# Message passing on one core: row limits compared on VectorE straight from PSUM, two transposes moved from TensorE to DMA, and a new instruction order

## The chip, the cores and the metric

The kernel runs on one core of a Trainium2 chip. The metric is the device time of one launch in microseconds, given as the median of several runs. One further execution was recorded by the hardware profiler. All durations of single instructions below come from that execution.

The core has five instruction streams. TensorE (PE in the profile; its weight loads are listed apart, as PEld) multiplies matrices and writes to PSUM. VectorE (DVE) and ScalarE (ACT) work elementwise and can read PSUM. GpSimd (POOL) works elementwise on SBUF. SyncE (SP) only issues DMAs here. Each stream executes its own instructions strictly in the order in which the program emits them, and waits on semaphores where it needs another stream's result.

## What is computed

There are 128 graphs of 128 nodes with 64 features. The reference, cut to what matters:

```python
# layer 0, per graph
mask = adj > 0
h  = relu((x @ W1a)[:, None, :] + (x[:, None, :] - x[None, :, :]) @ W1b + b1)   # node pair (j, k), 192 wide
hm = sum over k of h[j, k] * mask[j, k]
x  = layernorm(x + hm @ W2 + deg[:, None] * b2)          # deg = row sums of mask
# layer 1, per graph
m   = relu(relu(x @ V1 + c1) @ V2 + c2)
msg = relu(adj @ m)
x   = layernorm(x + GRU(msg, x))                          # three gates, 64 wide each
```

The mask is sparse: a row's neighbours are picked one by one, and only the picked pairs are computed.

## The kernel before

**Groups.** The 128 graphs are worked off in 32 groups of four (`G = 4`). For a group, `masks`, `ranks`, `degrees` and `counts` make the 0/1 mask, a running count of neighbours along each row (`rankT`), the row sums and, for each row, how many extra segments it needs (`nseg`). `values0` and `pieces` project `x` (the second one into three bf16 pieces `b0`, `b1`, `b2`).

**Picking neighbours.** Each row has a fixed number of first slots (`W0 = 8`, in two halves) and, where it has more neighbours, extra segments of `W1 = 4` slots. `pick0` builds 0/1 selection matrices on VectorE by comparing `rankT` with slot numbers. `gather0` multiplies these with the pieces on TensorE: 12 small matmuls a step and 16 steps a group. Each result lies in a PSUM tile `pv` that ScalarE has filled beforehand with the row's own part (`seed0`). `keep0` on ScalarE and `reduce` on VectorE (line 666, `acc`) apply the relu and add the results up. `pick1`, `gather1`, `seed1`, `keep1` and `reduce1` do the same for the extra segments. There are three `pv` buffers.

**Offsets, owners and places.** The extra segments of all rows are packed one after the other. `offsets` multiplies `nseg` by triangular matrices, which gives in PSUM (`po`) each row's first and last position. ScalarE copies the last position to `off` (line 458) and scales the first into `woff` (line 460). GpSimd then compares a ramp `iota` with `off`, once for each of the four graphs (`till`, line 466). A further matmul (`pp`) turns `till` into `own`, the 0/1 matrix that says which row owns a segment, and ScalarE copies `own` out twice (bf16 and f32).

`turned` transposes `rankT` with four TensorE transposes (`pr`, line 487) and copies the result to `rank` on ScalarE (line 490). `places` uses `rank`, `own` and `woff` (TensorE, `ps`, lines 504 to 511; ScalarE, `place`). `owners` transposes `own` in the same manner (`pq`, line 495; `ownT`, line 498), and `sums` uses `ownT` to add the segments' sums onto their rows.

**The rest.** `together` and `joined` (GpSimd) add the partial sums; `second` to `update` are layer 0's second matrix, the layernorms, layer 1 and the gates. The result of a group is stored by SP at the end of `update` (line 743).

**PSUM.** Apart from the three `pv` buffers there is a pool `ps_w` of two buffers with one tag, `w`. Every other matmul result passes through these two in turn: `pc`, `pd`, `po`, `pp`, `pr`, `pq`, `ps`, `pu`, `pz`, `ph`, `pw`, `pt`, `pm`, `pn`, `pa` and `pg`. The next matmul to use a buffer waits until the former content has been read.

**Order.** The order of the whole program is written out. Every step of every part of a group (a part is a generator, a step runs to its next `yield`) has a number in `TIMETABLE`. A step of group g has the time g times 100000 plus that number. Steps are emitted in the order of these times, and so interleave about six groups on every engine:

```python
for t in sorted(plan):
    for run in plan[t]:
        next(run, None)
```

`FIRST` and `SETUP` give other numbers for the first group and for the constants. The numbers fix an order and no durations.

Of the kernel before, what the change touches and what calls it, by code (L numbers as in the profile page):

```python
# [8 lines left out]
F32 = mybir.dt.float32  # L9
BF16 = mybir.dt.bfloat16  # L10
I32 = mybir.dt.int32
AF = mybir.ActivationFunctionType
ALU = mybir.AluOpType
AX = mybir.AxisListType

N = 128
# [3 lines left out]
G = 4  # L20
# [8 lines left out]

PER = 100000  # L30
TIMETABLE = {
    "load": (-268618,), "masks": (-266066,), "ranks": (-232900, -232900), "degrees": (-257102, -254423),
    "turned": (-224742, -220574), "counts": (-234901,), "offsets": (-217678, -211964, -197704, -192380, -189932),
    "owners": (-35894, -35894), "places": (-179586, -177714),
    "pieces": (-221915, -212465, -212465, -212025, -212025, -210034, -207896, -206287, -204509, -201502, -201502),
    "others": (-93885, -63613), "values0": (-168677, -168312, -168312), "pick0": (-187243, -177588, -157318, -147219),
    "pick1": (-101562, -99096), "over0": (-86465, -86465), "over2": (-91716, -89070), "base0": (-71690,),
    "base1": (-115079,), "base2": (-74898,), "base3": (-66289,), "together0": (-90368, -86071, -54801),
    "sums0": (-16639, -16639, -6895), "joined0": (-42043,), "joined2": (-9054,),
    "together1": (-31159, -22707, -22707), "together2": (-54332, -29252, -26680), "sums2": (-10324, -7550, -6743),  # L40
    "together3": (-14410, -11697, -11388), "second": (1322, 1729, 6614, 12070, 12714, 14947), "turn": (17589, 19125),
    "message1": (22148, 22871), "message2": (24221, 25357), "message3": (34134, 47496),
    "gates": (52002, 52335, 59212, 59212, 60471, 61641),
    "update": (63484, 134926, 134926, 146356, 147450, 212137, 231447, 236648, 276814),
    "seed0": (-137838, -111380, -107532, -90909, -89996, -88760, -70167, -48540),
    "gather0": (-132826, -123102, -109699, -102053, -101463, -95122, -90696, -82750, -82750, -77811, -77618, -69952,
        -66122, -48012, -38905, -32104), "keep0": (-129922, -97944, -81962, -65602),
    "reduce": (-116740, -102949, -100299, -89511, -89215, -81357, -75312, -71801, -69013, -44762, -33692, -24596),
    "seed1": (-80653, -43141), "gather1": (-77673, -72671, -67801, -55447, -41338, -33923, -28108, -20295),
    "keep1": (-76545, -38998), "reduce1": (-70927, -59829, -52180, -31003, -23063, -16037),  # L50
}


SETUP = (-227883, -212853, -185033, -155144, -101231, 22249)
FIRST = {
    "load": (-236749, -176840), "masks": (-192323,), "ranks": (-160512, -153527), "degrees": (-172354, -159518),
    "turned": (-108605, -102394), "counts": (-146837,), "offsets": (-115482, -109556, -106790, -103472, -99536),
    "places": (-98687, -93949),
    "pieces": (-169807, -166786, -164278, -164278, -164278, -164278, -158634, -152826, -143767, -142875, -113691),
    "values0": (-148521, -139633, -130220), "pick0": (-141784, -133982, -133982, -103074), "pick1": (-92485, -74065),  # L60
    "over0": (-88306, -87641),
}


# [1 line left out]
def adj_resnorm_kernel(  # L66
# [19 lines left out]
    nc = tc.nc  # L86
# [6 lines left out]
    ident_h = const.tile([N, N], BF16, name="ident_h")  # L93
# [13 lines left out]
    iota = const.tile([N, N], BF16, name="iota")  # L107
# [24 lines left out]
    def each(t, n):  # L132

        return t.rearrange("p (o c) -> p o c", o=1).to_broadcast([t.shape[0], n, t.shape[1]])
# [95 lines left out]
    def wide(t, n, w=F):  # L230
        return t.rearrange("p (g o) -> p g o", o=1).to_broadcast([N, n, w])
# [152 lines left out]
    with ExitStack() as fast:  # L384
        loads = fast.enter_context(tc.tile_pool(name="loads", bufs=4))
        prep = fast.enter_context(tc.tile_pool(name="prep", bufs=2))
# [3 lines left out]
        ps_w = fast.enter_context(tc.tile_pool(name="ps_w", bufs=2, space=bass.MemoryType.PSUM))  # L390
# [19 lines left out]
        def prep_parts(s):  # L410
            g = s["g"]
# [39 lines left out]
            def offsets():  # L451

                p = ps_w.tile([N, 2, G], F32, tag="w", name=f"po{g}")
                for c, m in enumerate((strict, incl)):
                    nc.tensor.matmul(p[:, c, :], m, s["nseg"], start=True, stop=True)
                yield
                off = prep.tile([N, G], F32, tag="off", name=f"off{g}")
                nc.scalar.copy(off, p[:, 1, :])  # L458
                s["woff"] = prep.tile([N, G], BF16, tag="woff", name=f"woff{g}")
                nc.scalar.mul(s["woff"], p[:, 0, :], 2.0 * W1)  # L460
                yield


                s["till"] = prep.tile([N, G, N], BF16, tag="till", name=f"till{g}")
                for i in range(G):
                    nc.gpsimd.tensor_scalar(s["till"][:, i, :], iota, off[:, i : i + 1], None, ALU.is_lt)  # L466
                yield
                p = s["po"] = ps_w.tile([N, G, N], F32, tag="w", name=f"pp{g}")
                nc.tensor.matmul(p, step, s["till"], start=True, stop=True)
                yield  # L470
                s["own"] = prep.tile([N, G, N], BF16, tag="own", name=f"own{g}")
                nc.scalar.copy(s["own"], s["po"])
                s["own32"] = prep.tile([N, G, N], F32, tag="own32", name=f"own32_{g}")
                nc.scalar.copy(s["own32"], s["po"])  # L474
# [7 lines left out]

            def turned():

                p = ps_w.tile([N, G, N], BF16, tag="w", name=f"pr{g}")
                for i in range(G):
                    nc.tensor.transpose(p[:, i, :], s["rankT"][:, i, :], ident_h)
                yield
                s["rank"] = prep.tile([N, G, N], BF16, tag="rank", name=f"rank{g}")
                nc.scalar.copy(s["rank"], p)  # L490

            def owners():
                p = ps_w.tile([N, G, N], BF16, tag="w", name=f"pq{g}")
                for i in range(G):
                    nc.tensor.transpose(p[:, i, :], s["own"][:, i, :], ident_h)
                yield
                s["ownT"] = prep.tile([N, G, N], F32, tag="ownT", name=f"ownT{g}")
                nc.scalar.copy(s["ownT"], p)

            def places():  # L500

# [62 lines left out]
            def pieces():  # L564
# [16 lines left out]

            return {
                "masks": masks, "ranks": ranks, "degrees": degrees, "counts": counts, "offsets": offsets,
                "turned": turned, "owners": owners, "places": places, "pieces": pieces, "others": others,
                "pick0": pick0, "pick1": pick1, "values0": values,
            }
# [159 lines left out]
        name, g, run = "setup", -1, setup(ps_g, ps_w)  # L746
        for t in SETUP:
            plan.setdefault(t, []).append(run)
        for g in range(ng):
            s = states[g]  # L750
# [24 lines left out]
    with ExitStack() as slow:  # L775
# [10 lines left out]
        with tc.If(flag > N):  # L786
            with tc.For_i(0, NB, 1) as b:
                bs = bass.ds(b, 1)

                s = {"name": "d", "adjT": one.tile([N, G, N], F32, name="d_adjT")}  # L790
# [23 lines left out]
                for c in range(2):  # L814
                    k = cs[c].stop
                    for what, at in ((u, c * N), (v, H + c * N)):
                        p = ps_o.tile([N, N], F32, tag="d", name="d_p")
                        nc.tensor.matmul(p[cs[c]], wall[0:F, at : at + k], dxT[:, 0, :], start=True, stop=True)
                        t = one.tile([k, N], F32, name=f"d_uv{at}")
# [5 lines left out]
                    t = one.tile([k, N], F32, name=f"d_nu{c}")  # L825
# [12 lines left out]
                for c in range(2):  # L838
                    t = one.tile([cs[c].stop, N], F32, tag=f"nd{c}", name="d_nd")
# [52 lines left out]
```

## Time and profile before

| | |
|---|---|
| median of 3 runs | 966.71 us (966.35 to 967.72) |
| profiled execution: time | 966.97 us |
| profiled execution: span, first to last instruction | 965.2 us |
| PE busy | 907.4 us, 94% of the span |
| DVE busy | 827.3 us, 86% |
| ACT busy | 841.4 us, 87% |
| POOL busy | 840.7 us, 87% |
| granted TensorE clock, mean | 0.980 of full speed |
| DMA, mean rate | 25 GB/s |

In the profile a "group" is all instructions of one line, engine and shape, with their number, busy time and mean duration in ns. An entry such as `<-PE pv L636` names what ended the idle time before an instruction. "issue" is idle time that nothing in the profile explains. SPq is SP's DMA queue.

### The profile page before, as it was taken

How to read it: one execution, taken by the hardware profiler on the slowest of the kernel's cores; microseconds unless marked ns; L12 is line 12 of the kernel's file. 1: busy time of each engine (PE TensorE's matmuls, PEld its weight loads, DVE VectorE, ACT ScalarE, POOL GpSimd, SP SyncE). 2: the span in 40 equal slices, each digit the busy share in tenths (PEclk: the TensorE clock that was granted, in tenths of full speed). 3: DMA queues.
4: the chain of work that ended last, by engine and by line, in shares of the span. 5: the costliest groups of instructions: out<-in, count | busy, mean ns of one | idle time of the engine just before them, and what ended most of it. 6: DMA issues, size and time to landing. Idle time of an engine off the chain costs nothing.

```text
span 965.2 us, 32667 instructions
## 1 busy us (share of the span) xinstructions
PE 907.4 (94%) x13333; PEld 723.1 (75%) x13335; DVE 827.3 (86%) x1586; ACT 841.4 (87%) x1762; POOL 840.7 (87%) x1233
## 2 busy tenths in 40 slices
PE   6888999999999999999999999999999999999984
PEld 3567777777877777878777787777778777777762
DVE  5687898888899888889988888988888898888962
ACT  3787899999999999999999999999999999999863
POOL 4576899999999999999999999999999999999774
PEclk6898999999999999999999999999999999999998
DMA  3000001111100111110001111011101001010000
GB/s 97 24 3 23 24 2 29 30 29 30 29 18 13 30 30 29 30 30 10 22 29 30 30 30 29 2 30 30 30 29 29 25 7 30 29 30 8 7 7 19
DMA packets 25565, 23.91 MB, mean 25 GB/s; under 512 B 4156, under 2 KB 21314, under 8 KB 25410
## 3 DMA queue, kind: packets, MB, share of 16 engines
q1 hardware_dynamic: 25410, 21.78, 7.9%
q8 instruction: 106, 1.74, 0.8%
q14 instruction: 49, 0.40, 0.1%
HBM read 17.57 MB, written 4.19 MB: 23 GB/s over the span
## 4 chain that ended last, share of the span: by engine, by line
PE 68%; ACT 14%; DVE 13%; issue 3%; POOL 1%; DMA 0%; SPq 0%; ACTq 0%; DVEq 0%; POOLq 0%
PE pv L636 32%; DVE acc L666 7%; ACT x L269 4%; PE ph L718 3%; PE pw L284 3%; PE pv L577 3%; ACT pv L606 3%; DVE pick L532 3%; ACT us L623 2%; PE pv L547 2%; PE pu L547 2%; PE ph L723 2%; PE ph L711 2%; PE pm L307 2%; PE pa L327 2%
## 5 line engine op out<-in xcount | busy, mean ns | idle before, releaser
L666 DVE SCALAR_TENSOR_TENSOR acc<-pv,acc 128x768 f32<-128x768 f32 x576 | 534.4, 952 | 102.6 <-PE pv L636 90.4
L636 PE MATMUL pv<-b,pick 64*128 64x192 bf16 x9216 | 465.9, 245 | 21.0 <-DVE acc L666 17.0
L636 PEld LDWEIGHTS <-pick 64*128 64x128 bf16 x9216 | 379.2, 95 | 92.9 <-issue 69.9
L606 ACT COPY pv<-u 128x768 f32<-128x768 f32 x256 | 206.3, 816 | 1.1 <-DVE acc L666 1.0
L656 ACT ACTIVATE acc<-pv 128x768 f32<-128x768 f32 x192 | 155.9, 812 | 17.1 <-PE pv L636 16.9
L686 POOL TENSOR_TENSOR acc<-acc 128x384 f32<-128x384 f32 x128 | 143.7, 1123 | 12.9 <-DVE acc L666 12.9
L466 POOL TENSOR_SCALAR till<-iota,off 128x128 bf16<-128x128 bf16 x128 | 100.3, 801 | 7.8 <-ACT off L458 7.8
L574 ACT CAST b<-pv 128x384 bf16<-128x384 f32 x192 | 83.0, 486 | 19.7 <-PE pv L547 10.5
L691 POOL TENSOR_TENSOR fs<-acc,nb 128x192 f32<-128x192 f32 x128 | 75.9, 593 | 21.6 <-ACT nb L678 14.1
L699 POOL TENSOR_TENSOR acc<-acc 128x384 f32<-128x384 f32 x64 | 77.8, 1216 | 7.3 <-DVE acc L666 7.2
L688 POOL TENSOR_TENSOR acc<-acc 128x192 f32<-128x192 f32 x128 | 77.9, 608 | 2.6
L518 DVE TENSOR_TENSOR pick<-rankT,ramp 128x2048 bf16<-128x2048 bf16 x64 | 77.2, 1208 | 0.7 <-POOL npad L448 0.7
L606 ACT COPY pv<-us 128x768 f32<-128x768 f32 x64 | 51.4, 803 | 26.4 <-DVE acc L666 26.4
L259 POOL TENSOR_SCALAR ve<-mv 128x4 f32<-128x4 f32 x64 | 39.5, 617 | 35.5 <-DVE mv L256 35.4
L263 POOL TENSOR_TENSOR rs<-ve,nhalf 128x4 f32<-128x4 f32 x64 | 66.8, 1043 | 0.0
L415 POOL TENSOR_SCALAR maskT<-adjT 128x512 bf16<-128x512 f32 x32 | 61.2, 1912 | 6.1 <-DMA adjT<-in_adjT_dram 6.0
L617 PE MATMUL pz<-u,own 128*128 128x192 f32 x256 | 57.7, 348 | 0.9 <-ACT own L474 0.9
L678 ACT ACTIVATE nb<-u,npad 128x192 f32<-128x192 f32 x128 | 58.5, 458 | 0.0
L532 DVE TENSOR_TENSOR pick<-pick 128x1024 bf16<-128x1024 bf16 x64 | 50.4, 787 | 0.0
L269 ACT ACTIVATE x<-y,nm,rs 128x64 f32<-128x64 f32 x128 | 45.9, 432 | 4.8 <-POOL nm L265 4.8
L269 ACT ACTIVATE o<-y,nm,rs 128x64 f32<-128x64 f32 x128 | 45.9, 446 | 2.2 <-POOL nm L265 2.2
L617 PEld LDWEIGHTS pz<-u,own 128*128 128x128 f32 x256 | 39.8, 189 | 9.3 <-ACT own L474 5.9
(148 smaller groups left out, 1635.6 us busy)
## 6 DMA issues: line engine op xcount, KB each, us to landing
adjT<-in_adjT_dram SPq DMA_DIRECT2D x32, 256.0 KB, 3.0
xT<-in_xT_dram SPq DMA_DIRECT2D x64, 64.0 KB, 2.7
x<-in_x_dram SPq DMA_DIRECT2D x32, 128.0 KB, 2.3
out_dram<-o SPq DMA_DIRECT2D x32, 128.0 KB, 1.7
wab<-in_w_dram SPq DMA_DIRECT2D x2, 96.0 KB, 2.9
bi<-in_b_ih_dram SPq DMA_DIRECT2D x1, 96.0 KB
bias<-in_b_hh_dram SPq DMA_DIRECT2D x1, 96.0 KB
wx<-in_w_hhT_dram SPq DMA_DIRECT2D x2, 48.0 KB, 2.7
```

The costliest lines, as they stand in the source:

```text
L269: nc.scalar.activation(s[into][:, i, :], y[:, i, :], AF.Identity, bias=nm[:, i : i + 1], scale=rs[:, i : i + 1])
L466: nc.gpsimd.tensor_scalar(s["till"][:, i, :], iota, off[:, i : i + 1], None, ALU.is_lt)
L532: nc.vector.tensor_tensor(v[:, q, 1], v[:, q, 1], v[:, q, 0], ALU.subtract)
L574: nc.scalar.copy(b[c][:, h::2, :], ps[h])
L606: nc.scalar.copy(v, src.to_broadcast(list(v.shape)))
L617: nc.tensor.matmul(p[:, i, :], s["own32"][:, i0 + i, :], s["u"][:, i0 + i, :], start=True, stop=True)
L636: nc.tensor.matmul(v[:, h, j, :], pick[ks], s[f"b{c}"][ks, gr, :], start=False, stop=c == 2, skip_group_check=True,)
L656: nc.scalar.activation(kept(s, t, i), view(s["pv", t, i, 0]), AF.Relu)
L666: nc.vector.scalar_tensor_tensor(out=a, in0=view(s["pv", t, i, k // CH if t == 0 else 0]), scalar=0.0, in1=a, op0=ALU.max, op1=ALU.add,)
L686: nc.gpsimd.tensor_tensor(f[:, 0], f[:, 0], f[:, 1], ALU.add)
L688: nc.gpsimd.tensor_tensor(f[:, 0, 0], f[:, 0, 0], f[:, 0, 1], ALU.add)
L699: nc.gpsimd.tensor_tensor(f[:, 0], f[:, 0], f[:, 1], ALU.add)
```

## The change

It has four parts.

- `offsets`: ScalarE's copy `off` and GpSimd's four compares are replaced by one VectorE instruction for all four graphs, which reads the positions from PSUM.
- `turned`: the four TensorE transposes and ScalarE's copy are replaced by one transposing DMA from `rankT` to `rank`, issued by SP.
- `owners`: the four TensorE transposes are replaced by one transposing DMA into a bf16 tile `ownTh` (one buffer). ScalarE's cast to `ownT` stays and reads this tile in place of PSUM.
- All numbers of `TIMETABLE`, `SETUP` and `FIRST` are new, so that the order on every engine is another one.

The diff, with the tables cut to the entries that the prediction speaks of:

```diff
 TIMETABLE = {
-    "load": (-268618,), "masks": (-266066,), "ranks": (-232900, -232900), "degrees": (-257102, -254423),
-    "turned": (-224742, -220574), "counts": (-234901,), "offsets": (-217678, -211964, -197704, -192380, -189932),
-    "owners": (-35894, -35894), "places": (-179586, -177714),
+    "load": (-314315,), "masks": (-311269,), "ranks": (-281416, -279535), "degrees": (-308187, -306446),
+    "turned": (-216977, -18671), "counts": (-281475,), "offsets": (-278362, -266464, -265598, -235959, -228391),
+    "owners": (-114645, -103252), "places": (-216789, -211240),
...
-    "together1": (-31159, -22707, -22707), "together2": (-54332, -29252, -26680), "sums2": (-10324, -7550, -6743),
+    "together1": (-94218, -93539, -86531), "together2": (-94335, -73037, -68500), "sums2": (-55924, -50305, -47321),
...
-    "gates": (52002, 52335, 59212, 59212, 60471, 61641),
-    "update": (63484, 134926, 134926, 146356, 147450, 212137, 231447, 236648, 276814),
+    "gates": (8385, 8385, 8385, 9129, 11738, 16452),
+    "update": (29284, 59775, 77080, 90142, 95754, 98858, 188885, 191998, 237400),
...
-    "keep1": (-76545, -38998), "reduce1": (-70927, -59829, -52180, -31003, -23063, -16037),
+    "reduce1": (-105273, -102912, -99738, -80132, -70830, -63420),
...
-SETUP = (-227883, -212853, -185033, -155144, -101231, 22249)
+SETUP = (-333823, -264135, -222944, -213662, -154103, -8690)
...
                     nc.tensor.matmul(p[:, c, :], m, s["nseg"], start=True, stop=True)
                 yield
-                off = prep.tile([N, G], F32, tag="off", name=f"off{g}")
-                nc.scalar.copy(off, p[:, 1, :])
                 s["woff"] = prep.tile([N, G], BF16, tag="woff", name=f"woff{g}")
                 nc.scalar.mul(s["woff"], p[:, 0, :], 2.0 * W1)
                 yield
                 s["till"] = prep.tile([N, G, N], BF16, tag="till", name=f"till{g}")
-                for i in range(G):
-                    nc.gpsimd.tensor_scalar(s["till"][:, i, :], iota, off[:, i : i + 1], None, ALU.is_lt)
+                nc.vector.tensor_tensor(s["till"], each(iota, G), wide(p[:, 1, :], G, N), ALU.is_lt)
                 yield
...
             def turned():
-                p = ps_w.tile([N, G, N], BF16, tag="w", name=f"pr{g}")
-                for i in range(G):
-                    nc.tensor.transpose(p[:, i, :], s["rankT"][:, i, :], ident_h)
-                yield
                 s["rank"] = prep.tile([N, G, N], BF16, tag="rank", name=f"rank{g}")
-                nc.scalar.copy(s["rank"], p)
+                nc.sync.dma_start_transpose(s["rank"], s["rankT"].rearrange("p g n -> p (g n)"))
+                yield

             def owners():
-                p = ps_w.tile([N, G, N], BF16, tag="w", name=f"pq{g}")
-                for i in range(G):
-                    nc.tensor.transpose(p[:, i, :], s["own"][:, i, :], ident_h)
+                t = prep.tile([N, G, N], BF16, tag="ownTh", name=f"ownTh{g}", bufs=1)
+                nc.sync.dma_start_transpose(t, s["own"].rearrange("p g n -> p (g n)"))
                 yield
                 s["ownT"] = prep.tile([N, G, N], F32, tag="ownT", name=f"ownT{g}")
-                nc.scalar.copy(s["ownT"], p)
+                nc.scalar.copy(s["ownT"], t)
```

## The prediction

> **What bounds the kernel now.** I read the page first, for the load of each engine.
>
> ```profile
> PE 907.4 (94%) x13333; PEld 723.1 (75%) x13335; DVE 827.3 (86%) x1586; ACT 841.4 (87%) x1762; POOL 840.7 (87%) x1233
> ```
>
> All four compute engines are nearly full, PE most. The chain of waits in order of time shows how regular the middle is: the same PE step (`pw`, first half) recurs with the same distance.
>
> ```profile
> 151.32 1.03 PE pw L284 x8
> ...
> 179.62 1.03 PE pw L284 x8
> ...
> 207.91 1.03 PE pw L284 x8
> ```
>
> The distance is 28.29 us: one group, one period. From the first group to the last there are 31 periods, 31 x 28.29 = 877.0 us. The remaining 88.2 us of the 965.2 us span are ramp and drain. So I work out one period and multiply by 31. The busy times of one period come from the table of windows (columns: window, length, PE, PEld, DVE, ACT, POOL busy, clock, DMA share, GB/s):
>
> ```profile
> 300.00:328.29 28.29, 27.68 (x420) 22.29 (x418) 25.49 (x49) 26.10 (x56) 26.32 (x40) 1.00 0.09 26
> ```
>
> The granted clock is 1.00. PE is idle for only 0.61 us of 28.29; DVE for 2.80, ACT for 2.19, POOL for 1.97. The waits of that window say who waits for whom:
>
> ```profile
> PE pv L636 <- DVE acc L666: 0.4, 1, 0.4
> DVE acc L666 <- PE pv L636: 2.4, 3, 1.8
> ```
>
> DVE waits for PE far more than PE for DVE. PE sets the period, so what leaves PE's queue shortens it, as long as no other engine fills up.
>
> **What leaves PE.** Busy times of matmuls overlap, so I count in PE's queue, from the end of the weight loads before a step to the start of the next step's:
>
> ```profile
> 422.51 1.14 PEld L636 LDWEIGHTS <-pick 64*128 64x128 bf16 x24
> 424.00 0.23 PEld L495 LDWEIGHTS <-own 128*128 128x128 bf16 x4 [0.36 <-DVE n L356]
> 424.33 0.45 PEld L636 LDWEIGHTS <-pick 64*128 64x128 bf16 x12
> ...
> 425.26 1.43 PEld L636 LDWEIGHTS <-pick 64*128 64x128 bf16 x36 [0.23 <-issue]
> 426.85 0.23 PEld L487 LDWEIGHTS <-rankT 128*128 128x128 bf16 x4 [0.16 <-issue]
> 427.18 0.44 PEld L636 LDWEIGHTS <-pick 64*128 64x128 bf16 x12
> ```
>
> `pq`: the loads before end at 422.51 + 1.14 = 423.65, the next gather starts at 424.33: 0.68 us, of which 0.36 is a wait for DVE's `n` to free a `ps_w` buffer. `pr`: 425.26 + 1.43 = 426.69 to 427.18: 0.49 us. Together 1.17 us a period. PE alone would then allow 28.29 - 1.17 = 27.12 us.
>
> A page of the Trainium skill speaks against this part. "VectorE: DVE Perf Modes", section "The three transpose paths", gives 390 ns for a 128x128 bf16 transpose on TensorE and 1309 ns by DMA, and advises TensorE where PSUM may be the target. The trace differs: four in a row hold the queue for 0.49 us, 0.12 each. By the page's figure the eight would free 8 x 0.39 = 3.1 us a period, and the kernel would fall by some 97 us as an estimate, which the other engines' load forbids.
>
> **What the other engines gain and lose.** The prices are these groups:
>
> ```profile
> L666 DVE SCALAR_TENSOR_TENSOR acc<-pv,acc 128x768 f32<-128x768 f32 x576 | 534.4, 952 | 102.6 <-PE pv L636 90.4
> L466 POOL TENSOR_SCALAR till<-iota,off 128x128 bf16<-128x128 bf16 x128 | 100.3, 801 | 7.8 <-ACT off L458 7.8
> L356 DVE TENSOR_TENSOR n<-pg,rh 128x128 f32<-128x128 f32 x64 | 18.7, 292 | 2.2
> L490 ACT COPY rank<-pr 128x512 bf16<-128x512 bf16 x32 | 18.7, 586 | 1.1 <-PE pr L487 1.0
> L498 ACT CAST ownT<-pq 128x512 f32<-128x512 bf16 x32 | 18.5, 577 | 0.0
> L458 ACT COPY off<-po 128x4 f32<-128x4 f32 x32 | 6.3, 198 | 0.0
> ```
>
> - DVE gains the compare `till`, 128x512 with one operand in PSUM, for which there is no row. The nearest rows that read PSUM are `n` (128 wide, 292 ns) and `acc` (768 wide, 952 ns): (952 - 292) / 640 = 1.03 ns an element, so 292 + 384 x 1.03 = 0.69 us. Ends: 0.35 us if it ran at the rate of the bf16 `pick` compare (2048 wide in 1208 ns, which makes 0.30, plus a little), 1.17 us if it cost four times `n`. I take 0.69, as both its rows read f32 from PSUM. DVE: 25.49 + 0.69 = 26.18 us.
> - ACT loses `off` and `rank`: 0.20 + 0.59. `ownT` now reads SBUF: between 0.58 as now and, from its SBUF rows `nb` (192 wide, 458 ns) and `pv<-u` (768 wide, 816 ns), 0.66. I take 0.66: 26.10 - 0.79 + 0.08 = 25.39 us.
> - POOL loses the four compares: 100.3 / 32 = 3.13 us, leaving 23.2 us. POOL was not the bound, so this gives no time by itself.
> - `ps_w` has two tenants fewer per group, but `po` is now held until DVE has run `till`. In the new order `till` (34402 in the period) stands between the fifth and sixth `reduce1` step, while PE does `ph`, the projections of `pieces` and a gather. In the old order DVE's wait of 1.8 us lies in just such a stretch, when PE turns from gathers to `po`, `ph` and the subtractions of `pieces`. I count `till` as covered by that wait; without the cover it costs up to 0.69 us.
>
> **What SP gains.** Two DMAs a group enter SP's queue, ahead of the next loads and behind the store, which waits for ACT:
>
> ```profile
> SPq L743 <- ACT o L269: 250.4, 10, 25.4
> ```
>
> That is ten periods: SP stands about 25 us of each period at the store. Modulo 100000 the new order on SP is store 37400, `turned` 83023, `owners` 85355, `load` 85685. `places`, which needs `rank` on PE, is 83211. Behind the store, the transpose's sources are already there: `rankT` is written at 20465 of the same period, `own` over a period before. So it goes out when the store does. From 37400 to 83211 PE has eight gather steps (0.6 us each), the `ph` steps (2.6), the subtractions (1.0), `pw` (1.7), `pp` (0.4) and `pz` (1.8): about 12 us for issue and landing. `masks` (88731) and the cast of `ownT` (96748) come later still.
>
> No row shows a transposing DMA. Lower end: `x`, 128 KB like this tile, lands in 2.3 us. Upper end, if each 2-byte element went as a packet: queue 1 used 7.9% of 16 x 965.2 us for 25410 packets, 48 ns each, and 65536 x 48 / 16 = 197 us. I take some 3 us, by `x` and by `adjT` (256 KB, 3.0 us). It is then hidden, and the loads move back by as much, also hidden. In the ramp, `load` of group 2 now stands behind `owners` of group 0, hence behind ACT's `own` (29 us into the trace) where it was issued at 20.4; its mask is due after `places` (30 us), so I allow 3 us either way for ramp and drain and take 0.
>
> **The sum.** The stall that goes with `pq` will partly return: after the gates both `ps_w` buffers wait for ACT and DVE, and the next tenants are now `pc` and `po`, with only two gathers before `pc`. I put the whole 0.36 us back: 27.12 + 0.36 = 27.48 us. DVE would be busy 95% of it. That saves 0.81 us a period, 31 x 0.81 = 25 us: 966.97 - 25.1 = 941.9 for the profiled execution. The median of before is 0.3 lower, so I say 942.
>
> **Rivals.**
> - *VectorE becomes the bound* (slower). DVE's idle 2.80 us is then no slack but the price of its round trips with PE and the three `pv` buffers, and stays; `till` comes on top. The period is 26.18 + 2.80 = 28.98, or + 0.69 x 31 = 21 us: 988. It decides from the point where more than 2.11 us of DVE's idle time survive; between that and 2.80 lies 967 to 988. For it: PE, DVE and ACT are all tightly coupled. Against it: DVE's waits are for PE's queue, which gets shorter.
> - *The transposes land late* (slower). If issue and landing take over 12 us, PE stands at `places`, with all later gathers behind it. Each us beyond costs up to 31 us, so one us makes 942 + 31 = 973. For it: nothing measured of such DMAs. Against it: five times the landing of `x` would be needed.
> - *No change.* ACT, POOL's round trips or the new order give back all 1.17 us: 966 to 968. The new order is then worse by itself, which only its trace can show.
> - *The floor.* The stall does not return, and the 0.4 us wait on `acc` goes too: 28.29 - 1.17 - 0.4 = 26.7, which gives 918 to 930.
>
> **How the numbers follow.** About 0.2% (2 us) is what a measurement of this kernel can tell from no change. Forecast, 930 to 961: 0.60. Floor, below 930: 0.06. No change: 0.05. VectorE: 0.20. Late transposes: 0.09. Faster is 0.66, same 0.05, slower 0.29. The range for 8 in 10 runs from 928 to 980: it leaves out some 0.04 below, and above it half of VectorE's case and of the late transposes', 0.14. The likeliest case alone has 930 to 961, which is a period between 27.1 and 28.1 us.
>
> **What would show it.** Right: `pw` recurs every 27.3 to 27.7 us; `till` on DVE lasts about 0.69 us with little idle before it; POOL loses some 100 us busy; `places` has no wait for a DMA; `pc` waits for `n`. Wrong: DVE above 96% of a period or PE's waits on `acc` grown above 1 us a period (VectorE); `ps` waiting for `rank` from a DMA, or SP's store no longer its long wait (late transposes).

## The result and the profile after

The changed kernel takes 969.55 us (median of 8 runs, 968.19 to 970.07); the kernel before, run beside it on the same chip, 966.31 us (965.64 to 967.72). The ratio is 1.0031, with a 95% interval of 1.002 to 1.0042: slower by 0.3%. The prediction said 942 us and gave 0.29 to "slower"; its range of 928 to 980 holds the result only by the room that it left for its rivals. The profiled execution of after took 969.54 us, its span 967.8 us.

The busy times, from the page of after:

```profile
PE 893.0 (92%) x13076; PEld 714.0 (74%) x13079; DVE 847.7 (88%) x1618; ACT 833.7 (86%) x1698; POOL 759.0 (78%) x1105
```

PE has 14.4 us less work than before and POOL 81.7 us less, DVE 20.4 us more. The work did move; the end did not come sooner. The recurrence of `pw`, from the timeline of PE in after:

```profile
144.87 1.10 PE L285 MATMUL pw<-w2c,hmT 128*128 128x64 f32 x8
...
173.46 1.10 PE L285 MATMUL pw<-w2c,hmT 128*128 128x64 f32 x8
...
202.06 1.10 PE L285 MATMUL pw<-w2c,hmT 128*128 128x64 f32 x8
```

The period is 28.59 us, where it was 28.29 and 27.48 was predicted. The table of windows over ten periods (columns: window, length, PE, PEld, DVE, ACT, POOL busy, clock, DMA share, GB/s), first of before, then of after:

```profile
300.00:582.94 282.94, 276.86 (x4164) 222.76 (x4162) 253.23 (x481) 260.92 (x551) 264.44 (x381) 1.00 0.09 25
```

```profile
300.00:585.94 285.94, 273.93 (x4085) 221.15 (x4083) 260.83 (x491) 259.24 (x531) 239.04 (x341) 1.00 0.14 34
```

Per period, before to after: PE is idle for 0.61, then 1.20 us; DVE is busy for 25.32, then 26.08 us, and idle for 2.97, then 2.51 us. So the 0.30 us by which the period grew is DVE's 0.76 us more of work less the 0.46 us by which its holes shrank. (Such a sum holds for every engine, and names no cause.) The waits in those ten periods, PE's of before, then PE's, DVE's and SP's of after:

```profile
PE pv L636 <- DVE acc L666: 3.6, 10, 0.4
...
PE pv L630 <- DVE acc L660: 3.6, 10, 0.4
PE pv L571 <- ACT b L568: 3.5, 10, 0.3
PE pv L630 <- ACT acc L650: 2.0, 10, 0.2
...
DVE acc L660 <- PE pv L630: 18.8, 30, 1.1
...
SPq L737 <- ACT o L270: 226.3, 10, 23.0
```

The list of PE's matmuls had one wait before (for `acc`, 0.36 us a period); it now has two more, both for ScalarE. (The weight loads, PEld, have a list of their own, with waits for ScalarE in both kernels.) SP still stands 22.6 us of each period at its store, so it has the time to issue the two transposes.

The whole difference of the spans, 2.6 us, has four parts, from ACT's `hmT` steps: the first comes at 52.54 us and not 56.99 (-4.5), the distance to the second is 32.59 and not 35.79 (-3.2), the next 28 distances sum to 800.6 and not 793.2 (+7.4), and the last two distances with the rest up to the end sum to +2.8. The better start hides most of what the steady periods lose.

### The profile page after: what moved, and what is told of

Read it like the earlier page. It is cut to its first block, busy times and chain, and to the rows that moved or that the text cites. A ratio compares the mean times of both kernels' runs of the same rounds, so it can differ in the third digit from the quotient of the medians.

```text
span 967.8 us, 32064 instructions
## 1 busy us (share of the span) xinstructions
PE 893.0 (92%) x13076; PEld 714.0 (74%) x13079; DVE 847.7 (88%) x1618; ACT 833.7 (86%) x1698; POOL 759.0 (78%) x1105
## 5 line engine op out<-in xcount | busy, mean ns | idle before, releaser
L630 PEld LDWEIGHTS <-pick 64*128 64x128 bf16 x9216 | 384.7, 94 | 108.6 <-issue 87.3
L512 DVE TENSOR_TENSOR pick<-rankT,ramp 128x2048 bf16<-128x2048 bf16 x64 | 89.0, 1392 | 0.0
L416 POOL TENSOR_SCALAR maskT<-adjT 128x512 bf16<-128x512 f32 x32 | 49.1, 1535 | 7.6 <-DMA adjT<-in_adjT_dram 7.6
L368 POOL TENSOR_TENSOR ub<-ua,rz 128x256 f32<-128x256 f32 x31 | 53.5, 1726 | 0.0
L571 PE MATMUL pv<-b,minus 128*128 128x384 bf16 x128 | 37.2, 334 | 10.7 <-ACT b L568 10.7
L712 PEld LDWEIGHTS ph<-ownT,acc 128*128 128x128 f32 x256 | 34.9, 190 | 15.8 <-POOL t L477 9.7
```

Source lines behind the costliest of these rows:

```text
L512: nc.vector.tensor_tensor(s[name][:, rows], s[src].rearrange("p (o g) n -> p o g n", o=1).to_broadcast([N, n, G, N]), ramp[:, first : firs ...
L630: nc.tensor.matmul(v[:, h, j, :], pick[ks], s[f"b{c}"][ks, gr, :], start=False, stop=c == 2, skip_group_check=True,)
```

## The experiments

Theory 1: the operations gain what was predicted and the new order loses it again. Theory 2: VectorE is the price (the first rival). Theory 3: what left PE was never on the path. Theory 4: PE's transposes stood in holes in which PE would else wait for ScalarE. Theory 5: the new order puts waits for ScalarE and VectorE on PE's way. Theories 6 and 7 came later and are told where they enter. Periods below are the median distance of one step between groups in the steady part.

### The parts one by one

**Only the two DMA transposes, in the old order.** `turned` and `owners` as in after, with `owners` (the DMA, then the cast) at its own places:

```
-    "owners": (-35894, -35894),
+    "owners": (-130000, -35894),
```

(`FIRST` gets such an entry of its own for the first group.)

> Before with the other part alone: both transposes by DMA, the compare stays on GpSimd, the old order else. Theory 1: most of the gain is here, 940 to 955. Theory 2: the same, 940 to 955, but then new_ops_old_order is slower than this by about 20 us. Theory 3: 964 to 968.

967.79 us; ratio 1.0008 (0.9998 to 1.0018), no difference that can be told; the period is 28.289 us. PE's queue has lost `pq`, `pr` and four changes between 64*128 and 128*128 weights, and nothing is gained. Its timeline shows what stands in their place (the last gathers behind the gates, where `pq` and `pr` were):

```profile
535.52 1.17 PE L632 MATMUL pv<-b,pick 64*128 64x192 bf16 x24
537.15 0.67 PE L632 MATMUL pv<-b,pick 64*128 64x192 bf16 x12 [0.46 <-ACT acc L652]
...
539.89 0.34 PE L632 MATMUL pv<-b,pick 64*128 64x192 bf16 x4 [0.15 <-ACT acc L652]
```

PE waits for ScalarE's `acc` at just these two points. In the kernel before, the waits of PE's matmuls over the ten periods name ScalarE nowhere; here they do, with 0.57 us a period:

```profile
PE pv L632 <- ACT acc L652: 5.7, 17, 0.5
PE pv L632 <- DVE acc L662: 3.6, 10, 0.4
```

The transposes stood where PE would have waited anyway. That is theory 4. The kernel before shows how close it was: ScalarE's `acc` behind the gates ends at 423.48 + 0.81 = 424.29, and the gather behind `pq` starts 0.05 us later.

```profile
423.48 0.81 ACT L656 ACTIVATE acc<-pv 128x768 f32<-128x768 f32 x1
424.34 0.67 PE L636 MATMUL pv<-b,pick 64*128 64x192 bf16 x12
```

Here, where PE does wait, it is 0.06 us (536.28 + 0.81 = 537.09, then 537.15). So this gather could not have come sooner whatever left PE's queue before it.

**A quarter of the transposes.** Only the first of the four in each step stays, ScalarE spreads it over the others; `rank` and `ownT` are then those of the first graph for all four:

```
-                for i in range(G):
+                for i in range(1):
...
-                nc.scalar.copy(s["rank"], p)
+                nc.scalar.copy(s["rank"], each(p[:, 0, :], G))
```

> Before with one TensorE transpose in place of four in turned and in owners; ScalarE's two copies keep their size and read that one four times over, so rank and ownT are right for the first graph of each group alone. Only PE's work changes: six transposes of 0.1 us a period go. Theory 4 (PE's transposes stood in holes where PE would else wait for ScalarE to empty a pv buffer; ways through ScalarE are as long): the period stays within 0.1 us of 28.29, the time is 963 to 968, and the wait for ScalarE's acc before the next gather appears. Rival (PE's queue sets the period): 0.6 us a period, 945 to 952.

967.55 us, ratio 1.0006 (0.9996 to 1.0016), period 28.283: PE's work was cut without any DMA, any new order or any change of VectorE, and it bought nothing. Time and period are as theory 4 expected; the new wait for `acc` isn't in PE's list of waits, but the timeline has it: `acc` ends at 423.38 + 0.81 = 424.19 and the gather starts at 424.25. Six transposes are some 0.33 us of PE's queue, as an estimate from the next run, and not 0.6.

**Every transpose twice.** `for i in [*range(G)] * 2` in both steps.

> Before with every transpose of turned and owners done twice into the same place, 0.8 us more of PE's work a period, nothing else changed. Theory 4: PE's way was as long as ScalarE's, so what is added counts nearly in full: a period of 28.8 to 29.1 us, 980 to 992. If PE had slack there, nothing: 965 to 970.

979.79 us, ratio 1.0138 (1.012 to 1.0156), period 28.734, a little under the 28.8 to 29.1 that was expected. The weight loads of the two steps, from the timeline:

```profile
427.80 0.45 PEld L495 LDWEIGHTS <-own 128*128 128x128 bf16 x8 [0.36 <-DVE n L356]
428.36 0.44 PEld L636 LDWEIGHTS <-pick 64*128 64x128 bf16 x12
...
430.87 0.45 PEld L487 LDWEIGHTS <-rankT 128*128 128x128 bf16 x8 [0.16 <-ACT acc L656]
```

Eight loads take 0.45 us where four took 0.23 (the prediction's rows), so both steps together hold the queue for some 0.45 us more; the period grew by 0.44. So the 0.8 us in the expectation was too much, and what was added is paid in full. Together the three runs are the point of this case: what is added to PE's queue is paid in full, and what is taken out is not given back. That is how a kernel behaves in which PE is one of several paths of about the same length.

**Only the compare, in the old order.** `off` goes, `till` on VectorE, emitted where GpSimd's was due to find its data:

```
-"offsets": (-217678, -211964, -197704, -192380, -189932),
+"offsets": (-217678, -211964, -211900, -192380, -189932),
```

> Before with one part alone: the compare on VectorE right after woff, the transposes stay on TensorE, the old order else. Theory 1: within 4 us of before, as VectorE waits there anyway (962 to 970). Theory 2: VectorE's 0.68 us come on top of each period, 980 to 988.

969.04 us, ratio 1.0023 (1.001 to 1.0037), period 28.453: +0.16 us for an instruction of 0.68 us. VectorE's holes take most of it, not all. (ScalarE and GpSimd have less to do in this run, so the 0.16 us are the balance.)

**All three operations, in the old order.** The two edits above together.

> All three new operations in the order of before. Only two kinds of entries differ from the old tables: the compare on VectorE comes right after ScalarE's woff (it must read the PSUM buffer before its next tenant), and the DMA of owners goes out 0.94 of a period before the cast that reads it. Theory 1 (the new order lost what the operations gained): the period falls from 28.29 to between 27.1 and 27.9 us, the time to 942 to 957. Theory 2 (VectorE is the price): the period stays at or above 28.3, the time is 966 to 975. Theory 3 (the parts taken from PE were never on the path, and the order is neutral): 964 to 968.

968.63 us, ratio 1.0016 (1.0003 to 1.0029), period 28.387: +0.10 us against the transposes alone. The groups of this kernel show where the compare bites: the next tenant of `po`'s buffer is `ph`, and it waits for `till` (8.1 us in all, 0.25 a period). In after it doesn't (the row of L705).

```profile
L704 PEld LDWEIGHTS ph<-ident,fs 128*128 128x128 f32 x192 | 19.8, 140 | 8.8 <-DVE till L463 8.1 <-issue 0.7
...
L705 PEld LDWEIGHTS ph<-ident,fs 128*128 128x128 f32 x192 | 19.8, 140 | 10.5 <-issue 10.5
```

So of the 0.30 us by which the period of after grew, 0.10 come with the operations when the old order is kept, and another 0.21 with the order (28.594 - 28.387). These are two steps on one way from before to after, and no prices that hold in any order: the wait that goes with the 0.10 is gone in after. Theory 1 is refuted in its first half: there was no gain of the operations for the order to lose.

**The old operations in the new order.** Before's operations with after's tables; the steps of `turned` and `owners` had to be set where two PSUM buffers of `ps_w` are to be had: `turned` (-224000, -222000), `owners` (-111100, -110000).

> The operations of before in the new order. The two TensorE transposes are put where the two PSUM buffers allow it (rank shortly before places, owners shortly after places), as the new tables have no place for them. Theory 1: clearly slower than both, a period of 28.6 + 0.5 to 1.2 us, 980 to 1005. Theory 2: without VectorE's compare the new order gives 955 to 966. Theory 3: 967 to 975.

1119.05 us, ratio 1.1578 (1.1558 to 1.1599), period 33.4, outside what each theory expected. It says only that this order isn't made for transposes with a PSUM buffer and a turn on GpSimd; it can't be used to price the order.

### The holes and the new order

**The holes filled.** Only the DMA transposes, and the steps behind them drawn into the waits: `ranks` (PE's `pc`) from -232900 to -234000, and the cast of `ownT` from -35894 to -68400.

> only_dma_transposes with two steps moved: PE's pc ahead of the gather step that now waits for ScalarE's acc, and ScalarE's cast to ownT from between tanh and rankT to an idle place before the copies of u. Theory 4: PE's hole of 0.46 us is filled with work and the second one (0.15 us) closes, the period falls by 0.2 to 0.5 us, 950 to 961. Rival (VectorE or GpSimd set the period): 964 to 969.

965.44 us, ratio 0.9986 (0.9975 to 0.9997), period 28.246. This is the one version that beats both kernels, the one before by 1.3 us: 0.05 us a period out of the 1.17 that left PE's queue. Theory 4 had expected 0.2 to 0.5 us from filled holes and 950 to 961, so this half of it failed; the time lies where the rival had it (VectorE or GpSimd set the period, 964 to 969).

**The statistics moved in after.** The second layer norm's statistics on VectorE (`update`, sixth time) from 98858 to 134450, away from the `acc` steps.

> The changed kernel with one step of one engine moved: VectorE's statistics of the last layernorm (update, sixth step, 0.87 us) go from between two reduce steps, just ahead of the gates, to right behind the compare, a third of a period later. No operation is changed. Theory 5 (the new order puts work of VectorE and ScalarE on the way that PE waits for; the chain of after runs over VectorE for 5.4 us a period where that of before had 2.7): the period falls from 28.59 to between 27.9 and 28.4, 945 to 963. Rival (another way is as long, as in the old order): 966 to 971.

969.55 us, ratio 1.0032 (1.0019 to 1.0044), period 28.600: no change, as the rival of theory 5 had it. The run shows more than that, see "VectorE's busy time" below.

**One PE wait of after taken away.** The third `minus` step of `pieces` goes behind the `ownT` matmuls of `ph`: -252972 to -250194. Nothing else differs on any engine.

> The kernel after, with one step moved: the eighth step of `pieces` (the third `minus` matmul on PE) from -252972 to -250194, so that PE issues it behind the `ownT` matmuls of `ph` and not before them. In the trace of after PE waits there 0.35 us for ACT's `b` (L568), and the next `minus` follows it in another array form. Theory 5 (the new order puts waits for ACT on PE's way): the wait goes under the `ph` step; the period falls from 28.59 to about 28.25 us, and the kernel by some 0.3 x 31 = 10 us to about 959. Theory 2 (VectorE is the price): nothing changes, 969 to 970, since the step has nothing to do with DVE.

992.35 us, ratio 1.0261 (1.0246 to 1.0276), period 29.354. The wait for `b` is gone, and the kernel is some 23 us slower than after. Neither theory had that. The timeline of all engines in one period:

```profile
356.81 1.22 DVE L512 TENSOR_TENSOR pick<-rankT,ramp 128x2048 bf16<-128x2048 bf16 x1
356.94 1.14 POOL L266 TENSOR_TENSOR nm<-nm,rs 128x4 f32<-128x4 f32 x1
...
358.11 1.43 ACT L270 ACTIVATE x<-y,nm,rs 128x64 f32<-128x64 f32 x4 [1.01 <-POOL nm L266]
...
361.07 0.96 DVE L660 SCALAR_TENSOR_TENSOR acc<-pv,acc 128x768 f32<-128x768 f32 x1 [2.18 <-ACT place L508]
```

`nm`, the last and smallest step of the first layer norm on GpSimd (0.20 us alone), began 0.13 us after VectorE's `pick` and ended with it. ScalarE's `x` waited 1.01 us for it, all of ScalarE's queue behind it was late, and VectorE waited 2.18 us. In after, the same `nm` just slips through:

```profile
349.81 0.20 POOL L266 TENSOR_TENSOR nm<-nm,rs 128x4 f32<-128x4 f32 x1
349.95 1.21 DVE L512 TENSOR_TENSOR pick<-rankT,ramp 128x2048 bf16<-128x2048 bf16 x1
```

In the one `nm` starts 0.14 us ahead of the `pick`, in the other 0.13 us behind it: a shift by 0.27 us decides over 0.76 us a period. The `nm` of the second layer norm does fall under a `pick` in after (355.51, 1.19 us long), and nothing waits for it: what a collision costs depends on who waits.

**Three more moves.** After_one_swap, and `degrees`, `base0`, `offsets` moved: `degrees` -306446 to -306067, `base0` -101199 to -110667, `offsets` -278362 to -279399.

> The kernel after with the move of after_one_swap and three more: `degrees` second step -306446 to -306067 (DVE's `deg` behind one `acc` step), `base0` -101199 to -110667 (ACT's `nb` earlier), `offsets` first step -278362 to -279399 (`po` on PE before a gather). No instruction is added or removed. Theory 5: another 0.1 to 0.15 us a period, about 955. Theory 2: still 969, DVE has the same work.

996.77 us, ratio 1.031 (1.0297 to 1.0323), period 29.550; the same collision (`nm` 1.12 us).

**Theory 6 and its test.** The swap cost what it did through that collision. The second `pick0` step goes behind the next `acc` step: `-218030` becomes `-215400`. Theory 7 is the rival: the swap is bad by itself.

> after_one_swap (992.35 us) with one more step moved: the second `pick0` step (a bf16 compare on DVE) from -218030 to -215400, behind the next `acc` step instead of ahead of it. In after_one_swap that `pick` begins at 356.81 and GpSimd's `nm` (L266, the last step of the first layer norm) at 356.94, and `nm` takes 1.14 us where it takes 0.20 alone; ACT's `x` then waits 1.01 for it and VectorE's `acc` 2.18 behind ACT. Theory 6 (a GpSimd step that falls under a bf16 `pick` of VectorE stands still, and that collision on the layer norm's chain is what the swap cost): `nm` is 0.20 again, and the period falls by 0.8 to 1.1 us, to 28.2 to 28.6, the time to 957 to 970. Theory 7 (the swap itself is bad for PE or ACT): no change, 990 to 993.

969.39 us, ratio 1.0026 (1.0017 to 1.0035), period 28.565: 0.79 us a period back, about what theory 6 said. The timeline now:

```profile
350.49 0.20 POOL L266 TENSOR_TENSOR nm<-nm,rs 128x4 f32<-128x4 f32 x1
350.73 1.43 ACT L270 ACTIVATE x<-y,nm,rs 128x64 f32<-128x64 f32 x4
351.20 0.96 DVE L660 SCALAR_TENSOR_TENSOR acc<-pv,acc 128x768 f32<-128x768 f32 x1 [0.76 <-PE pv L630]
...
352.07 1.22 DVE L512 TENSOR_TENSOR pick<-rankT,ramp 128x2048 bf16<-128x2048 bf16 x1
```

But it is no faster than after (28.594), although PE's wait of 0.35 us for `b` is gone (its wait for `acc` on ScalarE rose from 0.20 to 0.45 us a period). VectorE now waits 0.76 us for PE, in the hole that the `pick` used to fill.

> after_four_moves (996.77 us) with the same move of `pick0`. Theory 6: about 0.9 us or more a period back, 28.1 to 28.6, 953 to 968. Theory 7: no change, 995 to 998.

977.29 us, ratio 1.0106 (1.0091 to 1.0122), period 28.835: 0.72 us back, less than the 0.9 that was expected, and the time is above 953 to 968.

> The kernel after with the move of `pick0` alone. There `nm` of the first layer norm ends at 350.01, 0.06 us after the `pick` has begun at 349.95, and is not held up (0.20 us), so theory 6 expects no gain from it there: 967 to 971. If the collisions of GpSimd's other steps with that `pick` (`ub` takes 1.80 us instead of 0.73) were on the path as well, some 5 to 20 us less.

978.79 us, ratio 1.012 (1.0105 to 1.0136), period 28.868. Theory 6 had 967 to 971: the move costs 0.27 us a period where there is no collision to remove. The same hole of VectorE (0.8 us before an `acc`) is opened here for nothing. `ub` and the second layer norm's `nm` are free of collisions in this run (0.73 and 0.20 us), and that gains nothing that can be seen. This was the first sign that VectorE's order is on the path too.

Four runs now make a square: after 28.594, the swap alone 29.354, the `pick` alone 28.868, both 28.565. With the `pick` behind, the swap shortens the period by 0.30 us, close to what theory 5 gave it. So theory 5 is neither shown nor refuted: PE's wait may be worth its time where no collision hides it. The two runs don't settle it either, as VectorE is busy for 0.21 us less in the second (26.45 and 26.24 us a period) through other collisions.

**Two searched orders.** A search over the timetable, in a model of the five queues that was fitted to the traces of the runs above, for the DMA transposes alone and for all three operations.

> Only the two DMA transposes (till stays on GpSimd, as in only_dma_transposes), with an order found by a search over the timetable in a model of the queues that was fitted to the traces of these runs. If the transposes' 1.17 us can be had at all by placing the steps (theory 4: the holes must be filled), the period falls by about 0.6 us against only_dma_transposes, to 27.7, and the time to about 948 to 952. If the loops through ACT and DVE are the floor whatever the order (theory 3), it stays within 965 to 968.

985.48 us, ratio 1.0193 (1.018 to 1.0206), period 28.745.

> All three new operations (as after), with an order and a first group found by the same search. If DVE's compare is a price of its own (theory 2), this stays behind dma_transposes_best_order by some 0.2 us a period; theory 4 and 5: a period of about 27.95 and, with a ramp that may differ by 5 us, 953 to 960. If new order and new operations are both neutral (theory 3), 965 to 968.

969.14 us, ratio 1.0021 (1.0012 to 1.0029), period 28.498. Both expectations failed. The model had no collisions between VectorE and GpSimd in it; in both profiles GpSimd's steps again fall under `pick` steps (`ub` takes 1.6 and 1.8 us, alone 0.73). The floor that these orders might reach was not found.

### The chain of the layer norm

Is the layer norm's chain on GpSimd the path also where nothing collides? `nm` = -mean (0.23 us, 0.31 from start to start) is moved from GpSimd to VectorE, behind `mv`, or done twice on GpSimd:

```
-            nc.gpsimd.tensor_scalar(nm, mv[:, :, 0], -1.0, None, ALU.mult)
+            nc.vector.tensor_scalar(nm, mv[:, :, 0], -1.0, None, ALU.mult)
```

> The kernel before with that instruction twice on GpSimd: its chain is 0.31 us longer in each layer norm. Theory 6: the period rises by 0.15 to 0.31 us, the time by 5 to 10 us, to 972 to 977. If PE or VectorE were the bound (GpSimd is idle 1.97 us of a period): 966 to 968.

972.15 us, ratio 1.0058 (1.0042 to 1.0073), period 28.497: 0.62 us more on GpSimd cost 0.20, in the range of theory 6 (972 to 977).

> The kernel before; in both layer norms `nm` = -mean (L261, 128x4, 0.23 us on GpSimd and 0.31 from start to next start) is computed by VectorE right behind `mv`, so that GpSimd's chain from `mv` to `x` has three instructions and not four. PE and ScalarE have the same work, VectorE some 0.15 us a period more. Theory 6 (the path of a period runs through the layer norm's chain on GpSimd): the period falls by 0.15 to 0.31 us, the time by 5 to 10 us, to 957 to 962. If PE or VectorE were the bound: no change to 0.15 x 31 = 5 us slower, 967 to 972.

978.94 us, ratio 1.0138 (1.0112 to 1.0163), period 28.76: slower by 0.47 us a period, where theory 6 had 0.15 to 0.31 faster.

> The kernel after with `nm` = -mean on VectorE, as in before_short_norm. Theory 6: the period falls by 0.15 to 0.31 us, the time by 5 to 10 us, to 960 to 965, below the kernel before. If PE or VectorE were the bound: 969 to 975.

986.75 us, ratio 1.0214 (1.0194 to 1.0234), period 29.186: slower than after by 0.59 us a period. GpSimd's queue is shorter by 0.62 us a period, and VectorE's longer by two small instructions. The timeline of before_short_norm shows the size of one: `mv` ends at 351.89, the next `acc` begins at 352.00 (the pipeline lets an `acc` begin 0.08 us before `mv` ends in the kernel before), so 0.19 us each and 0.38 a period.

```profile
351.53 0.36 DVE L256 BATCH_NORM_AGGREGATE mv<-stats 128x2 f32<-128x6 f32 x4
351.93 0.17 DVE L258 TENSOR_SCALAR nm<-mv 128x4 f32<-128x4 f32 x1
352.00 2.05 DVE L666 SCALAR_TENSOR_TENSOR acc<-pv,acc 128x768 f32<-128x768 f32 x2
```

And the waits over ten periods show whom it hits: ScalarE, which seeds the next `pv` buffer as soon as VectorE's `acc` lets it go. First before, then before_short_norm:

```profile
ACT pv L606 <- DVE acc L666: 8.5, 20, 0.5
```

```profile
ACT pv L606 <- DVE acc L666: 13.6, 30, 0.7
```

What is added to VectorE's queue here is paid in full and more: `acc` (VectorE) frees a `pv` buffer, ScalarE seeds it, PE gathers into it, VectorE adds it up. And the shorter chain wasn't used. In before ScalarE's `x` starts 0.12 us after `nm` has ended (354.31, then 354.43); in before_short_norm `nm` is ready 0.49 us ahead of it, and `x` follows ScalarE's copy `us`:

```profile
353.42 0.20 POOL L265 TENSOR_TENSOR nm<-nm,rs 128x4 f32<-128x4 f32 x1
...
353.74 0.47 ACT L623 COPY us<-pz 128x384 f32<-128x384 f32 x1
...
354.11 1.43 ACT L269 ACTIVATE x<-y,nm,rs 128x64 f32<-128x64 f32 x4
```

So the chain on GpSimd is, like PE, one of several: lengthening it costs, and what shortening it frees is met by ScalarE's queue. One rival stays open for the size: new collisions came with the move (the second layer norm's `rs` takes 1.85 us there and not 1.04), and no run prices them. Theory 6 holds for the collision; no run shows the layer norm's chain as the path that alone sets the period of before or after.

## Why the prediction was wrong

**What leaves PE's queue shortens the period: this step failed.** It stood on PE's small idle share (0.61 us) and on DVE waiting for PE more than PE for DVE. Both readings were right and neither proves a bound. Taking the work off PE was to be worth 0.81 us a period, 1.17 less the 0.36 put back. The only_dma_transposes and quarter_transposes runs take work from PE, and the period stays at 28.29 and 28.28 us; in the former, PE's idle time grows from 0.61 to 1.09 us (its row of windows: 271.97 us busy of 282.89) as waits for ScalarE open where `pq` and `pr` were. What stood there in the prediction's place is ScalarE: its `acc` had ended only 0.05 us before the gather behind `pq`. Only adding shows PE's price (double_transposes: 0.44 us for 0.45 us). A stretch with no wait tells that an engine's work just covers the other path, not that it is the longer one.

**The cost of `till`: size right, place half right.** 0.68 us on DVE against the 0.69 worked out from PSUM-reading rows. Its group in after:

```profile
L464 DVE TENSOR_TENSOR till<-iota,po 128x512 bf16<-128x512 bf16 x32 | 21.6, 676 | 5.4 <-ACT woff L459 5.4
L492 ACT CAST ownT<-ownTh 128x512 f32<-128x512 bf16 x32 | 19.7, 614 | 0.0
```

It was put at nothing, "covered by that wait". In the old order it costs 0.10 to 0.16 us a period, a seventh to a quarter of it; what it costs in the new order no run shows. `ownT` at 0.61 us lies between the stated 0.58 and 0.66. ScalarE as a whole is busy for 25.92 us and not 25.39: its instructions overlap in the trace (in before `acc` starts at 426.17, 0.12 us before `rankT` ends), so two durations can't simply be taken off.

**The transposes on SP: right.** They land in 2.5 and 2.3 us (3 us taken), `places` has no wait for a DMA, and the slack of 12 us was never touched. The issues of after (median us to landing) and its first queue:

```profile
rank<-rankT SPq DMA_TRANSPOSE x32, 2.5
ownTh<-own SPq DMA_TRANSPOSE x32, 2.3
...
q1 hardware_dynamic: 60226, 30.17, 12.3%
```

The page "VectorE: DVE Perf Modes" of the Trainium skill, section "The three transpose paths", gives 1309 ns for 128x128. Four such tiles in one DMA land here 2.5 and 2.3 us after the issue, where a plain load of the same bytes (`x`) takes 2.3; no run has one tile alone. The upper end of 197 us, one packet for each element, was far off: 34,816 more packets on the queue for 64 transposes are 544 each.

**The stall put back: right in kind, empty in effect.** `pc` does wait for `n` (0.37 us a period), which the prediction put back in full, but the 1.17 us that it was set against shortened nothing by leaving.

**GpSimd loses 100 us: 81.7 us in the profile.** The rest came back as collisions, on balance: `ub` now takes 1.73 us on the mean where it takes 0.73 alone, some 31 us in all, while `ve` and `maskT` got shorter.

**VectorE's busy time, 26.18 us: right by accident.** It is 26.08 by the window rows over ten periods, from 25.32 before. `till` explains 0.68 of the 0.76; beside it the new order makes the `pick` compares meet GpSimd's steps. The groups of new_ops_old_order, then of after, the same operations in the two orders:

```profile
L511 DVE TENSOR_TENSOR pick<-rankT,ramp 128x2048 bf16<-128x2048 bf16 x64 | 77.3, 1210 | 0.7 <-ACT rankT L425 0.7
L511 DVE TENSOR_TENSOR pick<-place,ramp 128x2048 bf16<-128x2048 bf16 x32 | 39.2, 1225 | 2.1 <-ACT place L507 2.1
```

```profile
L512 DVE TENSOR_TENSOR pick<-rankT,ramp 128x2048 bf16<-128x2048 bf16 x64 | 89.0, 1392 | 0.0
L512 DVE TENSOR_TENSOR pick<-place,ramp 128x2048 bf16<-128x2048 bf16 x32 | 45.2, 1413 | 0.0
```

Two compares by 0.18 us and one by 0.19 make 0.55 us a period; the subtractions give 0.20 back (788 to 687 ns, twice). That is the 0.35 us by which VectorE is busier in after (26.08) than in new_ops_old_order (25.73), and the period is longer by 0.21. The sizes look like VectorE as the price of the new order, but after_stats_moved speaks against it. There, with one step moved, the two `pick` compares from `rankT` take 1247 ns on the mean and not 1392, and VectorE is busy for 25.77 us a period, 0.31 less than in after; the period stays at 28.600. (A step of GpSimd, `t`, collides in their place.) Its row of windows:

```profile
300.00:586.00 286.00, 274.63 (x4084) 221.82 (x4080) 257.72 (x491) 259.31 (x531) 248.82 (x341) 1.00 0.13 34
```

New_ops_best_order has it the other way round: VectorE is busy for 26.48 us, and the period is shorter than that of after (28.498). So VectorE's busy time isn't shown to be what the new order costs.

**The rivals.** The nearest is VectorE: its condition was that more than 2.11 us of DVE's idle time survive, and 2.51 do; its band of 967 to 988 holds the result. That is little proof: with DVE busy for 26.1 us, more than 2.1 us of idle time is the same as a period above 28.2. The prediction's own signs of this rival are absent: DVE is busy for 91% of a period and not over 96%, and PE's wait on DVE's `acc` is 0.36 us as before and not over 1. What is shown is the 0.10 to 0.16 us of the compare in the old order. What argued against it, that DVE waits for PE's queue and that gets shorter, fell with the first step: PE's queue was shorter only in work. "No change" had the reason right in the main (the freed time is given back, to waits for ScalarE where the traces name one) and a range that ends 1.5 us too low. Late transposes and the floor are refuted.

**What stays open.** Which of the new order's moves costs the 0.21 us, and whether its five more changes of the weights' shape on PE (28 a period against 23 in new_ops_old_order, counted in the weight loads) have a part in it.

## What to carry to other kernels

An engine with no idle time in a hand-set schedule is not yet the bound: look for what it would wait for if its work were gone (here ScalarE's `acc`, just behind), and price a removal by that and an addition in full. When several engines are over 90% busy and feed each other through two or three buffers, test the bound in a single run by taking a piece of work out, before rebuilding the order. And look for small steps of one engine that start close to a long one of another that can block them: a shift by 0.27 us decided over 23 us.

## What the runs showed of the hardware

**VectorE and GpSimd hold each other up.** A GpSimd step that starts under a bf16 `pick` (two operands in SBUF) stands still until the `pick` ends: `nm` 1.14 us and not 0.20 (after_one_swap), `ub` 1.80 and not 0.73 (after). The other way round a `pick` that starts under a GpSimd step takes up to 1.6 us and not 1.2. Under `till`, with one operand in PSUM, GpSimd isn't held (after):

```profile
338.44 0.68 DVE L464 TENSOR_TENSOR till<-iota,po 128x512 bf16<-128x512 bf16 x1
338.84 0.59 POOL L682 TENSOR_TENSOR acc<-acc 128x192 f32<-128x192 f32 x1
```

That agrees with the page "SBUF — State Buffer" of the Trainium skill, section "Who interferes with whom": a VectorE instruction with two SBUF inputs contends with GpSimd instructions that read SBUF, and whoever is second waits. In the kernel before this was already to be seen: `ve` took 0.62 us on the mean there, and takes 0.23 in after, where nothing collides with it.

**At a change of the weights' shape PE's loads have a gap of about 0.16 us.** Between weight loads of the gathers (64*128) and of other shapes the profile has a gap with no releaser, between loads of one shape none. Two of them, in after:

```profile
330.06 0.42 PEld L328 LDWEIGHTS pa<-adjT,m 128*64 128x64 f32 x8 [0.16 <-issue]
330.64 0.90 PEld L630 LDWEIGHTS <-pick 64*128 64x128 bf16 x22 [0.17 <-issue]
```

In one period of the kernel before there are 27 such changes, and the gaps there (most of them 0.1 to 0.2 us, some with a wait for another engine in them) sum to 4.6 us of the weight loads' 28.29. What a gap costs is not shown: matmuls run on meanwhile (PE is idle for 0.61 us a period), and only_dma_transposes lost four changes and gained nothing.
